# Top-p attention on one core: feature sums on another engine, the odd tile's work rearranged, diffusion a tile further ahead

## The chip, the core and the metric

The kernel runs on one core of one Trainium2 chip, in a single launch. The metric is the device time of a run in microseconds (us). A core has engines that each run their own queue of instructions: TensorE (matmul; PE, with its weight loads as PEld), VectorE (DVE), ScalarE (ACT), GpSimd (POOL) and SyncE (SP, which here only issues transfers). They wait for each other through semaphores.

## The reference, cut to what matters

`x` has 3327 nodes of 256 features, `adj` is a 3327 x 3327 matrix, everything in float32. Four layers run one after the other, each as `x = layernorm(x + layer(x, adj))`: a GraphSAGE layer, a GCN with a Mamba block behind it, a GAT, and the layer that the change touches:

```python
def top_p_attention(X):                    # A: 3327 x 3327
    q, k = X @ W1.T @ W2.T, X @ W3.T       # 64 columns each
    probs = softmax(q @ k.T)
    # per row: sort, keep the largest until their sum reaches 0.9
    A = probs * keep
    return A / max(A.sum(-1), 1e-12)

R = adj + eye(N); R = R / R.sum(-1)
Z, Xf, Xa = 0, X, X
for n in range(2):
    A = top_p_attention(Xa)
    Xf = R @ Xf                            # "diffusion"
    Xa = A @ Xa                            # "values"
    Z = Z + Xf @ U1[n].T + Xa @ U2[n].T
out = layernorm(X + Z)
```

The two rounds of this loop are called the first and the second attention here.

## The kernel before, in words

**Tiles.** The nodes are padded to 3328 and cut into `nt` = 26 row tiles of 128; two neighbouring tiles make one of `nh` = 13 pairs. A row tile of attention needs a row `e` of 3328 logits for each of its 128 nodes, in one SBUF buffer (`e`, four of them).

**One row tile of the first attention** goes through these steps. `scores` (line 1141) yields four chunks of 832 logits: two matmuls into the PSUM tile `sc`, of which there is one buffer, then a copy to `e` on ScalarE (line 1160; line 1163 where the last chunk is uneven). GpSimd sets the padded last column (line 1146). `search_short` (line 1387) finds the row's threshold on VectorE: 26 MAX8 over 128 columns each, given out in five steps (four steps of 5, one of 6), then six rounds of MAX8 and MATCH_REPLACE over the 208 candidates; in the first round it also issues the exponential of the whole row on ScalarE (line 1404). Then come `crossing`, which sums the sorted candidates to find the threshold `v`, and two passes over half of `e` each, which zero what lies under `v`. Every `yield` is one step, and `look()` takes one step of the search at the head of `queue`; a look where the queue is empty does nothing.

**Pairs and products.** Diffusion and values of a pair of tiles multiply a 256-row block matrix with the features by a scheme with seven 128-wide products in place of eight (`products`, line 1165), which needs sums of blocks on both sides. `blocks` (line 1191) makes the four sums of the feature blocks once, in `t1` to `t4` (in the buffer `G`, which is not in use yet), with four VectorE operations of 128 x 1664. The sums on the other side are made per pair: `diffused_pair` (line 1224) loads parts of the adjacency (`at`, two groups of 128 columns of each half to a part, and sums stored in `mixed` by an earlier layer) and adds the rest (`cb`) on VectorE; it yields once after its first part and once after each of its 13 groups of products. `assembled` (line 1176) puts the seven results together (`c`, eight VectorE operations), and `with_own` adds the own part, which `own_part` put in `F` on GpSimd (line 1203). `attended_pair` (line 1252) does the same for the values: `turn` transposes four 128 x 128 blocks of `e` on TensorE into the PSUM tile `tp` (two buffers) and ScalarE copies it to `wt` (line 1263); `mix` makes four sums of it in `sw` with three VectorE operations; then come seven matmuls. It begins with three turns and two mixes before its first yield; after that each of 13 steps issues the turn three ahead, one mix and one step's products. In the traces the three turns at its start are read from the matmuls `tp<-ident,e`.

`first` (line 1550) closes a row tile: the value sums are scaled, transposed to `xt` (VectorE copy), multiplied with U1 and U2, and stored (`s`, `Y`, `G` and the keys of the second attention).

**What sets the order.** In the first attention `fixed` is true: the wrapper `Fixed` (lines 882 to 893, where most matmuls and VectorE operations are recorded under line 891) keeps TensorE and VectorE in the order in which the program issues their instructions. So the order is written out by hand in a loop over pairs, and one engine's instruction that waits holds everything behind it on that engine. ScalarE, GpSimd and SyncE are ordered by the framework's scheduler, except for single instructions that are pinned.

Each turn of the loop (lines 1726 to 1745) has four parts. (1) The *even stage*, 7 steps: at each step one step of the next pair's diffusion (`spread`), at every second step one chunk of logits of tile 2i+2, looks as `counts` says; step 0 ends the previous pair (`end_pair`), step 5 empties the search queue and starts the values of pair i (`attend_to`, with the three turns). (2) Seven steps of values, with one look in five of them. (3) The *odd stage*, 6 steps of diffusion, with logits of tile 2i+3 at every second step, the second tile's `first`, and looks of 2, 1, 2, 1, 2, 1; the search of tile 2i+2 is emptied at its end and that of tile 2i+3 appended. (4) Six steps of values; the diffusion's assembly comes after the first, and the looks are in the last four.

```python
stage(spread, 7, logits(2 * i + 2), ends, counts,
      {0: lambda: end_pair(i - 1) if i else None, 5: lambda: attend_to(i)})
counts = [1, 2, 2, 2, 2, 0, 0]
```

Ahead of the loop an opening does the diffusion of tile 1 alone with plain products (`diffused_first`), between the logits of tiles 0 and 1, with the first search beside it. `blocks` comes ahead of all this.

**The second attention** (lines 1778 to 1839) goes tile by tile: in iteration `i` (from -2) tile `i+2` gets its logits, tiles `i` and `i+1` are searched (`search_long`, mostly on ScalarE and GpSimd), tile `i-1` has its values, and one tile's diffusion (`diffused`, line 1302: loads of `at`, 26 matmuls, one VectorE operation into `xf`) is spread through the iteration. Here the scheduler orders VectorE and TensorE too, except for what is pinned. `DL` is 1, and `more = range(len(xfs), min(nt, i + DL + 1))` gives iteration `i` the diffusion of tile `i+1`, from i = -1 to 24. Four buffers `xf` hold the results.

## Time and profile before

| | |
|---|---|
| three runs | 3424.53, 3426.78 (median), 3435.73 us |
| the profiled execution, its own time | 3433.03 us |
| its span, first to last instruction | 3431.1 us |
| mean granted TensorE clock | 0.964 |
| PE busy | 3140.4 us, 92% |
| PEld busy | 2565.8 us, 75% |
| DVE busy | 2686.5 us, 78% |
| ACT busy | 1735.4 us, 51% |
| POOL busy | 1127.6 us, 33% |
| first attention, about 1690 to 2568 us of the span | PE 840.35 of 878 us |
| second attention, about 2568 to 3431 us | PE 805.10 of 863 us |

How to read the profile. It shows one profiled execution, and its times start at the first instruction. An engine is busy while it runs an instruction; what an idle engine waited for is inferred from the semaphore that came last. In a line of a timeline the columns are the start, the duration, the engine, the source line, the operation, output <- inputs, the shape, how often it was repeated, and in square brackets the idle time ahead of it with its releaser. A table of windows has, for each stretch, its length and then every engine's busy time with its number of instructions. "PE tp L891 <- DVE e L891" in a list of waits reads: TensorE, about to write `tp`, waited for VectorE's last work on `e`; then come the total, the number of waits and the longest.

### The profile page before, as it was taken

The numbers are of one execution on the slowest core, as the hardware profiler recorded it, in microseconds if no ns is written. First come the engines' busy times: TensorE is split into PE (matmuls) and PEld (weight loads), VectorE is DVE, ScalarE is ACT, GpSimd is POOL, SyncE is SP. The second block draws the span as 40 slices with busy tenths as digits, with TensorE's granted clock in tenths as the row PEclk, the third lists the DMA queues.
The fourth block names the chain that finished last, engine by engine and source line by source line (L and its number), as shares of the span: only waits on it lengthen the run. The fifth ranks groups of instructions, "written<-read, shape, count | busy, mean of one in ns | idle before, by whom it ended". The sixth has DMA issues, their size and how long they took to land. (4 is left out here: it accounts for less than half of the span.)

```text
span 3431.1 us, 50276 instructions
## 1 busy us (share of the span) xinstructions
PE 3140.4 (92%) x18301; PEld 2565.8 (75%) x18301; DVE 2686.5 (78%) x5895; ACT 1735.4 (51%) x2764; POOL 1127.6 (33%) x1332
## 2 busy tenths in 40 slices
PE   8999888898988776999989999999998999999996
PEld 5999657676675554888778888888885677777775
DVE  4655368999999997877578778778755898988886
ACT  1000456767767675111133333333337788888883
POOL 0000245666665654111400000000003566656563
PEclk9999999999999988999999999999998999999998
DMA  6775334334343322444322232232213122222220
GB/s 200 251 253 188 105 101 125 110 108 116 102 115 89 69 57 81 150 137 151 115 76 87 65 88 79 69 89 80 71 50 102 52 68 68 64 66 65 72 64 16
DMA packets 206264, 344.31 MB, mean 100 GB/s; under 512 B 22223, under 2 KB 129167, under 8 KB 205871
## 3 DMA queue, kind: packets, MB, share of 16 engines
q1 hardware_dynamic: 205998, 340.92, 33.2%
q8 instruction: 148, 2.42, 0.3%
q14 instruction: 118, 0.96, 0.1%
HBM read 304.65 MB, written 36.21 MB: 99 GB/s over the span
## 5 line engine op out<-in xcount | busy, mean ns | idle before, releaser
L330 POOL TENSOR_TENSOR h<-du,row 128x2048 f32<-128x2048 f32 (+1 forms) x110 | 465.5, 4232 | 344.9 <-DVE hc L330 248.6
L330 DVE TENSOR_TENSOR_SCAN h<-dA,carry,h 128x512 f32<-128x512 f32 (+1 forms) x384 | 449.0, 1220 | 18.2 <-ACT dA L337 18.1
L337 ACT ACTIVATE dA<-t,A_log 128x512 f32<-128x512 f32 (+1 forms) x448 | 292.5, 658 | 147.1 <-DVE h L330 145.5
L1296 PE MATMUL acc<-F,at 128*128 128x256 f32 x1352 | 354.3, 388 | 1.8 <-DMA at<-in_adjT 1.8
L1341 PE MATMUL acc<-G,wt 128*128 128x256 f32 x1352 | 336.6, 392 | 9.7 <-ACT wt L1139 9.3
L1341 PEld LDWEIGHTS acc<-G,wt 128*128 128x128 f32 x1352 | 250.1, 193 | 72.4 <-ACT wt L1139 42.2
L1079 PE MATMUL acc<-F,at 128*128 128x257 f32 x1352 | 303.4, 381 | 0.7 <-ACT r L1023 0.7
L389 PE MATMUL cb<-F,at 128*128 128x256 f32 x1196 | 295.5, 395 | 8.0 <-ACT hn L409 3.4
L1296 PEld LDWEIGHTS acc<-F,at 128*128 128x128 f32 x1352 | 239.3, 191 | 74.9 <-issue 46.6
L1146 POOL MEMSET e<- 128x1 f32 x52 | 4.9, 99 | 838.5 <-PE tp L891 769.5
L1079 PEld LDWEIGHTS acc<-F,at 128*128 128x128 f32 x1352 | 253.3, 190 | 36.2 <-issue 1.0
L680 PE MATMUL y<-ident,hc 128*128 128x128 f32 x1664 | 236.4, 296 | 46.2 <-DVE hc L330 46.1
L680 PEld LDWEIGHTS y<-ident,hc 128*128 128x128 f32 x1664 | 210.4, 154 | 87.4 <-DVE hc L330 62.6
L389 PEld LDWEIGHTS cb<-F,at 128*128 128x128 f32 x1196 | 229.8, 198 | 58.3 <-issue 19.4
L330 DVE TENSOR_TENSOR hc<-h,row 128x2048 f32<-128x2048 f32 (+2 forms) x114 | 243.2, 2135 | 11.3 <-PE y L680 4.3
L891 PE MATMUL acc<-X,at 128*128 128x128 f32 (+1 forms) x988 | 173.7, 287 | 6.0 <-issue 6.0
L1263 ACT COPY wt<-tp 128x512 f32<-128x512 f32 x156 | 90.8, 589 | 166.6 <-PE tp L891 153.2
L138 PE MATMUL acc<-t,cb 128*128 128x128 f32 (+1 forms) x1014 | 168.4, 275 | 0.0
L891 PEld LDWEIGHTS acc<-X,at 128*128 128x128 f32 x988 | 142.2, 193 | 29.9 <-issue 26.1
L891 PE MATMUL acc<-G,sw 128*128 128x128 f32 x936 | 155.5, 275 | 0.0
L891 DVE MAX8 cand<-e 128x8 f32<-128x128 f32 x676 | 139.8, 277 | 5.0 <-ACT e L1160 3.2
L1160 ACT COPY e<-sc 128x832 f32<-128x832 f32 x78 | 65.9, 845 | 149.2 <-PE sc L891 149.1
(414 smaller groups left out, 7263.0 us busy)
## 6 DMA issues: line engine op xcount, KB each, us to landing
at<-in_adjT SPq DMA_DIRECT2D x54, 832.0 KB, 4.5
at<-in_adjT SPq DMA_DIRECT2D x130, 320.0 KB, 3.0
row<-bc SPq DMA_DIRECT2D x80, 512.0 KB, 5.1
at<-in_adjT SPq DMA_DIRECT2D x52, 640.0 KB, 5.5
at<-in_adjT SPq DMA_DIRECT2D x52, 576.0 KB, 4.1
at<-in_adjT SPq DMA_DIRECT2D x72, 256.0 KB, 3.1
at<-mixed SPq DMA_DIRECT2D x72, 256.0 KB, 3.6
mixed<-cb SPq DMA_DIRECT2D x26, 640.0 KB, 4.2
```

The source lines that it names most:

```text
L138: mm = nc.tensor.matmul(acc, w[:, j, :], x, start=(y == 0 and k % 3 == 0 and k < 6), stop=(y == nh - 1 and k in (2, 6)))
L330: return lambda *x, **k: tc.keep_in_program_order(op(*x, **k))
L337: decays.append(op(*x, **k))
L389: ten.matmul(acc, at[:, j % JC, :], X0[:, j, :], start=(j == 0), stop=(j == nt - 1))
L680: x = ten.matmul(y[:, g * P:(g + 1) * P], h[:, g, i * P:(i + 1) * P], ident, is_transpose=True, start=(first and g == 0), stop=(last and g ...
L891: return lambda *x, **k: tc.keep_in_program_order(op(*x, **k))
L1079: nc.tensor.matmul(acc, at[:, j, :], F[:, j0 + j, :], start=(j0 + j == 0), stop=(j0 + j == nt - 1))
L1146: nc.gpsimd.memset(e[:, n:], NEG)
L1160: copy(halves[:, :, c0:c0 + ws[0]], pl[:, :, :ws[0]])
L1263: nc.scalar.copy(wts[-1], pt)
L1296: nc.tensor.matmul(acc, at[:, j, :], rhs[:, j0 + j, :], start=(j0 + j == 0), stop=(j0 + j == nt - 1))
L1341: tensor.matmul(acc, wt[:, j, :], rhs[:, j0 + j, :], start=(j0 + j == 0), stop=(j0 + j == nt - 1))
```

## The change

Five edits.

1. `blocks` issues its four subtractions on GpSimd.
2. `attended_pair` yields after its first turn, after its second turn and first mix, and after its third turn and second mix, in place of once after all of them. A new `go_on` takes the next of these steps.
3. `stage` counts the keys of `then` from its end and takes a new argument `every` (2 unless given) for the logits. Even stage: the values start at its sixth step, `go_on` comes in its seventh step and once more behind it (after the remaining logits and ends); its looks become 2, 2, 2, 1, 0, 0, 0. Odd stage: one chunk of logits at every step (four chunks in steps 0 to 3, each `scores` yield being a chunk), the search of tile 2i+3 is appended at step 4 and the looks are 2, 2, 2, 2, 3, 3, with no `finish` behind it. The last values of the pair have a look in steps 2 and 5 only.
4. In the opening two chunks of tile 0's logits are issued ahead of the first diffusion's first step, and `blocks` is called behind tile 0's logits.
5. In the second attention iteration `i` diffuses tile `i+2`, from i = -2 to 23, one tile to an iteration; `xf` has five buffers.

```diff
         def blocks(x, t):
...
-            vector.tensor_sub(t1, b12, b11)
-            vector.tensor_sub(t2, b22, t1)
-            vector.tensor_sub(t3, b22, b12)
-            vector.tensor_sub(t4, t2, b21)
+            for y, c, d in ((t1, b12, b11), (t2, b22, t1), (t3, b22, b12), (t4, t2, b21)):
+                nc.gpsimd.tensor_tensor(y, c, d, op=ALU.subtract)
...
         def attended_pair(quads, psum, es, b):
...
-            for j in range(3):
-                turn(j)
-            for j in range(2):
-                mix()
+            turn(0)
+            yield None
+            turn(1)
+            mix()
+            yield None
+            turn(2)
+            mix()
             yield None
...
         def diffused(work, atp, psum, p, it, out, each=J3):
...
-            d = work.tile([P, D], F32, name="xf", bufs=DL + 3)
+            d = work.tile([P, D], F32, name="xf", bufs=DL + 4)
...
-                b = blocks(X, [flat[:, k * nh * HD:(k + 1) * nh * HD].rearrange("p (t d) -> p t d", t=nh) for k in range(4)])
...
-                def stage(spread, steps, groups, ends, counts, then):
+                def stage(spread, steps, groups, ends, counts, then, every=2):
                     for k in range(steps):
                         next(spread, None)
-                        then.get(k, int)()
-                        if k % 2 == 0:
+                        then.get(k - steps, int)()
+                        if k % every == 0:
                             next(groups, None)
...
+                def go_on():
+                    next(turned[0])
...
                 groups = logits(0)
                 x = diffused_first(quads, psum, 1, xfs)
+                next(groups)
+                next(groups)
                 for _ in groups:
                     next(x)
+                b = blocks(X, [flat[:, k * nh * HD:(k + 1) * nh * HD].rearrange("p (t d) -> p t d", t=nh) for k in range(4)])
...
                 for i in range(nh - 1):
-                    stage(spread, 7, logits(2 * i + 2), ends, counts,
-                          {0: lambda: end_pair(i - 1) if i else None, 5: lambda: attend_to(i)})
-                    counts = [1, 2, 2, 2, 2, 0, 0]
+                    stage(spread, len(counts), logits(2 * i + 2), ends, counts,
+                          {-7: lambda: end_pair(i - 1) if i else None, -2: lambda: attend_to(i), -1: go_on})
+                    go_on()
+                    counts = [2, 2, 2, 1, 0, 0, 0]
                     queue.append(searches[2 * i + 2])
...
-                    stage(spread, 6, logits(2 * i + 3), todo[1], [2, 1, 2, 1, 2, 1], {})
-                    finish()
-                    queue.append(searches[2 * i + 3])
+                    stage(spread, 6, logits(2 * i + 3), todo[1], [2, 2, 2, 2, 3, 3],
+                          {-2: lambda: queue.append(searches[2 * i + 3])}, 1)
...
-                        looks(k > 1)
+                        looks(k in (2, 5))
...
-                    more = range(len(xfs), min(nt, i + DL + 1))
+                    more = range(len(xfs), min(nt, i + DL + 2, len(xfs) + 1))
```

## The prediction, made before the changed kernel had run

> **What bounds the kernel now.** I read the page first (busy shares), then the engines' busy time by stage, then TensorE's own waits, then the timeline of one pair of tiles on TensorE, VectorE and ScalarE. The change touches two stages: the first attention (about 1690 to 2568 us of the span) and the second (2568 to 3431).

> By stage, the columns are the window, its length, then busy time and instruction count of PE, PEld, DVE, ACT and POOL, the granted clock and the DMA:

> ```profile
> 1948.82:2014.12 65.30, 64.00 (x496) 56.96 (x496) 52.19 (x177) 24.17 (x39) 0.20 (x2) 1.00 0.27 79
> 2014.12:2471.26 457.14, 448.04 (x3472) 398.72 (x3472) 365.10 (x1233) 169.99 (x273) 1.38 (x14) 1.00 0.27 79
> ```

> The first attention repeats every 65.30 us, one pair of tiles (457.14 is seven of them), and TensorE works 64.00 us of that. So at most 1.30 us a pair can be won in the steady part. TensorE's waits say where it is (total, times, longest):

> ```profile
> PE tp L891 <- DVE e L891: 21.9, 13, 8.9
> PE sc L891 <- ACT e L1160: 3.1, 2, 2.2
> PE tp L891 <- ACT wt L1263: 2.6, 11, 0.2
> ```

> ```profile
> 2012.57 0.49 PE L891 MATMUL tp<-ident,e 128*128 128x128 f32 x3
> 2014.12 0.76 PE L891 MATMUL tp<-ident,e 128*128 128x128 f32 x5 [1.06 <-DVE e L891]
> 2015.13 0.66 PE L891 MATMUL tp<-ident,e 128*128 128x128 f32 x4 [0.24 <-ACT wt L1263]
> ```

> The three turns of a pair stand in a row; the fourth transpose needs the odd tile's search, which ends 1.06 us late, and the third turn waits 0.24 us for a PSUM buffer. Eleven pairs do this; the first waits 8.86 and 1.33 us. VectorE is 80% busy (52.19 of 65.30), so its order matters. This is the odd stage on VectorE:

> ```profile
> 1974.40 0.69 DVE L891 COPY xt<-tp 128x512 f32<-128x512 f32 x1 [3.76 <-PE tp L891]
> ...
> 1978.55 0.43 DVE L891 TENSOR_TENSOR s<-tp,X 128x256 f32<-128x256 f32 x1 [1.49 <-PE tp L891]
> ...
> 1984.44 0.42 DVE L891 TENSOR_TENSOR sw<-wt 128x256 f32<-128x256 f32 x1
> 1984.90 0.62 DVE L891 TENSOR_TENSOR sw<-sw,wt 128x128 f32<-128x128 f32 x2
> ...
> 1988.56 0.42 DVE L891 TENSOR_TENSOR sw<-wt 128x256 f32<-128x256 f32 x1
> ...
> 1993.09 2.99 DVE L891 MAX8 cand<-e 128x8 f32<-128x128 f32 x15
> ```

> It stands still before `xt` and `s`, waiting for TensorE, then runs without a break into the sums `sw` (mix 9 at 1984.44, mix 10 at 1988.56) that TensorE's products 9 and 10 use. On ScalarE an exponential sits ahead of a copy of logits:

> ```profile
> 1968.14 3.07 ACT L1404 ACTIVATE e<-e,neg 128x3328 f32<-128x3328 f32 x1 [1.95 <-DVE neg L891]
> 1971.21 0.83 ACT L1160 COPY e<-sc 128x832 f32<-128x832 f32 x1
> ```

> [...] while VectorE waits 3.76 us for `xt`, nothing behind it runs. [...] here the 8.86 us wait is followed by half clock, the 1.06 us ones are not. [...] a GpSimd sum of 256 columns (L1588) took 4.09 us beside a VectorE pass over e, against 0.72 us at its shortest. [...] the 2048-column rows of L330 took 4.23 on average.

> **Part by part, in the first attention.**

> Sums of blocks on GpSimd. Four operations of 1664 columns leave VectorE (2.07, 1.98, 1.88 and 2.08 us: 8.0 us, 1702.4 to 1710.4). [...] GpSimd is free of the layer before at 1692.4, earlier than VectorE, and the first product that reads them starts at 1732; the own parts that fill GpSimd now (23 in 26.5 us) would still end by 1733. VectorE gains almost nothing at once: after the sums it waits 0.79 us more for a transfer before `cb` at 1711.16, which stays ahead of the search. [...] if the memset of e's last column, now at 1718.8, slipped to 1733, the first search would slip with it. I take zero, with +4 us as the bad end.

> Opening order. With two groups of logits ahead of the diffusion's first transfer, tile 0's logits end some 5.5 us sooner (before, the last copy ended at 1719.2). But VectorE then meets `F` behind TensorE's last diffusion product (1728.95, gap 5.79), in both orders. By then the new order has five rounds of the search done instead of one, so four rounds of 0.85 us come off what is behind, plus the rest of the shift: 4 to 7 us sooner at the first turn. I take -5.

> Turns spread out. One turn, then a product, turn, logits, turn: the 0.24 us goes, and twelve transposes find their copies. That is -0.24 x 11.

> Search of the odd tile earlier. Its looks move from values' steps (four to two) and from the even stage (9 before the turn to 7), so 2.9 us of VectorE work (six MAX8 of 0.195 us, two rounds of 0.85) leaves the stretch before the turn, against a lateness of 1.06 us. The wait goes: -1.06 x 11. Together with the turns -14.3 us.

> What it costs. Four groups of logits now follow each other at every step of the odd stage. The second (TensorE ready at 1969.48 + 1.65 = 1971.13) needs the one PSUM buffer of logits, whose copy stands behind the 3.07 us exponential and ends at 1972.04: a wait of 0.95 us a pair, where now there is none. If ScalarE were ordered copy first, the exponential would hold the next copy for about 0.6, so 0.6 to 1.0.

> The larger one: steps 4 and 5 of the odd stage hold all 26 MAX8 of the odd tile's search (26 x 0.195 = 5.1 us), in VectorE's queue *ahead of mix 9*. Count from TensorE's start of the product at 1978.35. Now VectorE finishes mix 9 at +7.15 (1985.5), and TensorE needs it at +11.0 (product 9, 1989.37) plus 0.45. Afterwards VectorE does 5.1 more and 0.4 less (one MAX8 of a round moves ahead of `s`): +11.85. TensorE comes earlier, because two groups of logits of 0.98 moved ahead: product 9 starts at +9.05, and its fourth operand, the last sum of the mix, is due at +9.7. Wait 2.1 us. Then VectorE has the eight operations of `c` and the two of `F` (1985.43 to 1988.64, 3.2 us) before mix 10 (1.05): +16.0. TensorE, released at +11.85, is through with product 9 at +12.75 and needs mix 10 at +13.2. Wait 2.75 us. Mix 11 and 12 then come in time. The idle time before `xt` and `s` doesn't absorb the MAX8, since they stand behind both. Sum 0.95 + 2.1 + 2.75 = 5.8 us a pair in eleven pairs; in the first pair no `xt` or `s` stops VectorE, and the same count leaves 1.3.

> First attention: 11 x 5.8 + 1.3 - 14.3 - 5 = +46. If those waits are a third shorter (TensorE slower on the way, VectorE a little faster than I add up) it is +25. Two waits near 2.5 us within 6.5 may also cost half-clock stretches of 3.4 us, each worth 1.7: 0 to +15; I take none.

> **The second attention.**

> ```profile
> 2568.80:2639.20 70.40, 54.40 (x208) 35.09 (x208) 27.66 (x80) 51.07 (x42) 27.54 (x60) 0.84 0.41 128
> 3342.60:3373.30 30.70, 25.51 (x127) 20.73 (x126) 26.31 (x78) 21.05 (x20) 13.56 (x32) 0.96 0.13 39
> ```

> One tile of diffusion (52 halves of 0.22, 11.5 us) moves from the iteration at 3342 to the opening at 2568. At the end VectorE is busy 26.31 of 30.70 us, so taking 11.5 us from TensorE wins only about 3: what is late next is the search of the last tiles. The opening has 16 us of idle TensorE, so the tile fits, but TensorE and ScalarE run in order there: the first transfer is issued at 2571.7 and takes 3 to 5 us, so logits behind its products come up to 7 us later, and the first searches with them. A cost of 0 to 10; I take 6. Net +3. One more `xf` buffer costs no time. SyncE's queue issues the same loads, one iteration earlier.

> **Sum.** The profiled execution took 3433.0 us (span 3431.1 and 1.9 around it). 46 + 3 = +49 gives 3482; the median of the runs, 6.2 lower, gives **3476**.

> **Rivals.** (a) VectorE keeps up, because the 13 us it has free in each pair take the MAX8 in: the waits at products 9 and 10 stay away, the logits' wait too. For it: 80% busy; against it: the free time lies ahead of `xt` and `s`. Then -14.3 - 5 + 3 = -16: about 3411. It decides once VectorE enters the odd values less than 4 us behind TensorE. (b) A part: only product 9 or the logits wait, about 1.3 us a pair, which cancels the turn's gain: 3420 to 3437. (c) The sums on GpSimd come late and hold TensorE's first products and the search: up to +10 on top of the main case. (d) The second attention's opening loses nothing and its end wins 3: main case at 3467.

> **How the numbers follow.** Main case (with c and d inside it) 0.74, own range 3447 to 3500: low end +25 first attention with -3 in the second, high end with half-clock stretches. Rival a 0.17, b 0.09. The range 3418 to 3500 leaves out most of (a) and the main case's tail. About 0.3% (10 us) can be told from no change: faster 0.17, same 0.08, slower 0.75.

> **What would show it.** Right: a pair lasts 69 to 70 us instead of 65.30; the wait for e before the turn is gone; new waits of TensorE for `sw` of some 2 and 2.7 us in each odd stage's values, and of `sc` on ScalarE's copy near 0.95. Wrong: a period at 64.0, or VectorE's MAX8 of the odd tile lying in the gap ahead of `xt`. The opening is right if the first turn comes about 5 us sooner; the second attention if its first turn comes 6 us later after 2568 and its last iterations 3 us shorter.

## The result: slower by more than forecast

The changed kernel takes **3512.56 us** (median of four runs, 3511.76 to 3516.53), the kernel before 3427.79 us in the same comparison: a ratio of 1.0246, 95% interval 1.0227 to 1.0265. Forecast were 3476 us and a range of 3418 to 3500; the sign was right, the time lies above the range. The profiled span grew from 3431.1 to 3510.6 us.

First TensorE's waits in the first attention of the changed kernel (the total in us, times, longest):

```profile
PE acc L891 <- DVE sw L891: 39.9, 43, 1.9
PE sc L891 <- ACT e L1160: 27.4, 15, 14.4
PE acc L891 <- DVE cb L891: 5.2, 1, 5.2
PE tp L891 <- DVE e L891: 4.9, 2, 3.4
```

The wait for `e` ahead of the turn is gone from every pair (two are left, in the opening), and a wait for the sums `sw` has come in its place, as forecast. But a single wait for logits of 14.4 us is new as well; nothing of that kind was in the forecast's sum. This is TensorE and VectorE in one odd stage and the values behind it:

```profile
2065.26 0.97 PE L891 MATMUL sc<-kT,q 64*128 64x416 f32 x4 [0.78 <-ACT e L1160]
...
2079.93 5.12 DVE L891 MAX8 cand<-e 128x8 f32<-128x128 f32 x26
2084.97 0.41 DVE L891 TENSOR_TENSOR sw<-wt 128x256 f32<-128x256 f32 x1
...
2085.43 0.49 PE L891 MATMUL acc<-G,sw 128*128 128x128 f32 x2 [1.39 <-DVE sw L891]
...
2089.55 0.49 PE L891 MATMUL acc<-G,sw 128*128 128x128 f32 x2 [1.86 <-DVE sw L891]
```

The 26 MAX8 of the odd tile's search stand directly ahead of the sums `sw` that TensorE waits for. Now three pairs by stretch, from one odd tile's `xt` to the next:

```profile
1929.67:2000.37 70.70, 66.35 (x498) 58.90 (x498) 52.33 (x176) 24.34 (x40) 0.20 (x2) 0.98 0.25 72
2000.37:2069.50 69.13, 64.78 (x499) 57.33 (x498) 52.23 (x176) 24.41 (x40) 0.20 (x2) 1.00 0.26 74
2069.50:2138.58 69.08, 64.72 (x498) 57.27 (x498) 52.23 (x176) 24.36 (x40) 0.20 (x2) 1.00 0.26 74
```

A pair takes 69.1 us where the granted clock (third number from the end) stays at 1.00, and 70.7 to 71.0 where it drops to half for 3.41 or 6.83 us (half clock, below); it was 65.3. VectorE's busy time is the same as before (52.2 us), only its order is new.

Cut at four marks that both traces have, the added time lies here:

| stretch | before | after | added | forecast |
|---|---|---|---|---|
| first logits to the `xt` in the odd stage of the loop's second turn (opening, first pair) | 143.3 | 160.0 | **+16.6** | -5 |
| from there ten pairs, to the `xt` in the odd stage of the last turn | 653.1 | 701.5 | +48.4 | 10 x 4.5 = +45 |
| from there to the second attention's first logits | 71.9 | 75.4 | +3.5 | +5.8 |
| second attention's first logits to the first product of its values | 72.2 | 85.3 | **+13.1** | +6 |
| from there to the end | 790.1 | 789.7 | -0.5 | -3 |

With the first logits 1.7 us earlier in the new trace (a difference of the layers ahead, which the change doesn't touch) that is the 79.4 us of the span. The pairs came as forecast; the two openings did not.

**The opening of the first attention.** In the kernel before, GpSimd set the column in time, and TensorE's longest wait for the copy of logits was 2.17 us:

```profile
1718.81 0.18 POOL L1146 MEMSET e<- 128x1 f32 x4
1718.82 3.39 DVE L891 MAX8 cand<-e 128x8 f32<-128x128 f32 x17 [1.79 <-ACT e L1163]
1726.88 0.97 PE L891 MATMUL sc<-kT,q 64*128 64x416 f32 x4 [2.17 <-ACT e L1160]
```

GpSimd, VectorE, ScalarE and TensorE of the changed kernel, in this order:

```profile
1715.45 3.71 POOL L1196 TENSOR_TENSOR G<-X,G 128x1664 f32<-128x1664 f32 x1
1719.10 3.70 POOL L1196 TENSOR_TENSOR G<-X 128x1664 f32<-128x1664 f32 x1
1722.74 3.70 POOL L1196 TENSOR_TENSOR G<-G,X 128x1664 f32<-128x1664 f32 x1
1726.36 0.20 POOL L1146 MEMSET e<- 128x1 f32 x4
```

```profile
1726.52 0.30 DVE L891 MAX8 cand<-e 128x8 f32<-128x128 f32 x1 [12.16 <-POOL e L1146]
```

```profile
1727.53 3.07 ACT L1405 ACTIVATE e<-e,neg 128x3328 f32<-128x3328 f32 x1 [16.00 <-POOL F L1201]
1730.60 0.83 ACT L1160 COPY e<-sc 128x832 f32<-128x832 f32 x1
```

```profile
1715.05 1.99 PE L891 MATMUL acc<-X,at 128*128 128x256 f32 x8
1731.48 1.76 PE L891 MATMUL sc<-kT,q 64*128 64x416 f32 x4 [14.44 <-ACT e L1160]
```

It is a queue four engines long. A memset (0.20 us for four of them) stands behind three sums of 3.70 us in GpSimd's queue; the first sum stands ahead of the own parts, at 1691.1. The last of 26 MAX8 reads the column that it sets and waits 12.16 us for it. The exponential needs that MAX8 (it starts 0.12 us after `neg`, which the MAX8 leads to; GpSimd's next own part, which the profile names, merely ended later than `neg`), and the copy of the next tile's logits stands behind the exponential on ScalarE. TensorE needs the one PSUM buffer that this copy frees, and it runs in program order, so the diffusion's products behind the logits stand still too.

**The opening of the second attention**, on TensorE:

```profile
2635.58 0.97 PE L1154 MATMUL sc<-kT,q 64*128 64x416 f32 x4 [1.93 <-ACT q L907]
2645.68 2.90 PE L1297 MATMUL acc<-F,at 128*128 128x256 f32 x6 [9.13 <-DMA at<-in_adjT]
2648.51 1.76 PE L1154 MATMUL sc<-kT,q 64*128 64x416 f32 x4
```

After one chunk of tile 0's logits the first diffusion's products are next in TensorE's order; their load is issued at 2638.53, and they start at 2645.68. Tile 0's other chunks wait behind them: the second starts 12.9 us after the first, where it was 2.7 us before. In the kernel before, the diffusion came after tile 0's logits, and the load landed beside those:

```profile
2571.43 1.76 PE L1154 MATMUL sc<-kT,q 64*128 64x416 f32 x4 [0.99 <-ACT e L1139]
...
2581.31 5.14 PE L1296 MATMUL acc<-F,at 128*128 128x256 f32 x12
```

### The profile page after: what moved, and what is told of

Read it like the earlier page. It is cut to its first block, busy times and chain, and to the rows that moved or that the text cites. A ratio compares the mean times of both kernels' runs of the same rounds, so it can differ in the third digit from the quotient of the medians.

```text
span 3510.6 us, 50279 instructions
## 1 busy us (share of the span) xinstructions
PE 3163.3 (90%) x18301; PEld 2583.3 (74%) x18301; DVE 2678.9 (76%) x5891; ACT 1738.0 (50%) x2764; POOL 1136.5 (32%) x1336
## 5 line engine op out<-in xcount | busy, mean ns | idle before, releaser
L330 POOL TENSOR_TENSOR h<-du,row 128x2048 f32<-128x2048 f32 (+1 forms) x110 | 465.8, 4235 | 344.6 <-DVE hc L330 248.5
L330 DVE TENSOR_TENSOR_SCAN h<-dA,carry,h 128x512 f32<-128x512 f32 (+1 forms) x384 | 448.9, 1220 | 18.3 <-ACT dA L337 18.1
L1297 PE MATMUL acc<-F,at 128*128 128x256 f32 x1352 | 353.5, 388 | 11.2 <-DMA at<-in_adjT 11.1
L1342 PE MATMUL acc<-G,wt 128*128 128x256 f32 x1352 | 336.7, 392 | 13.2 <-ACT wt L1139 12.9
L330 DVE TENSOR_TENSOR hc<-h,row 128x2048 f32<-128x2048 f32 (+2 forms) x114 | 243.0, 2133 | 11.3 <-PE y L680 4.3
L891 PE MATMUL acc<-G,sw 128*128 128x128 f32 x936 | 163.1, 284 | 36.6 <-DVE sw L891 36.6
L891 PE MATMUL acc<-X,at 128*128 128x128 f32 (+1 forms) x988 | 176.6, 291 | 0.0
L891 PEld LDWEIGHTS acc<-X,at 128*128 128x128 f32 x988 | 143.9, 195 | 32.3 <-issue 27.5
L891 PEld LDWEIGHTS acc<-G,sw 128*128 128x128 f32 x936 | 134.9, 199 | 41.3 <-DVE sw L891 41.3
L891 DVE MAX8 cand<-e 128x8 f32<-128x128 f32 x676 | 137.7, 276 | 12.3 <-POOL e L1146 12.2
```

Of the source, the lines that this page charges most:

```text
L330: return lambda *x, **k: tc.keep_in_program_order(op(*x, **k))
L891: return lambda *x, **k: tc.keep_in_program_order(op(*x, **k))
L1297: nc.tensor.matmul(acc, at[:, j, :], rhs[:, j0 + j, :], start=(j0 + j == 0), stop=(j0 + j == nt - 1))
L1342: tensor.matmul(acc, wt[:, j, :], rhs[:, j0 + j, :], start=(j0 + j == 0), stop=(j0 + j == nt - 1))
```

## The experiments

Ratios are to the kernel before, run in the same comparison (its medians there were 3430.35 to 3431.86 us).

**E1 to E4 start from the changed kernel.** E1 puts the memset ahead of the sums; on TensorE, VectorE and ScalarE every instruction keeps its place in the order. (All four sums then stand behind the own parts, the first one too.)

```diff
-                nc.gpsimd.memset(e[:, n:], NEG)
+                first_memset.append(nc.gpsimd.memset(e[:, n:], NEG))
...
-                b = blocks(X, [...])
+                with tc.issue_after(first_memset[0].ins): b = blocks(X, [...])
```

> The changed kernel, with the memset of e's last column put ahead of the four sums in GpSimd's queue; nothing else moves. In the changed kernel the last MAX8 of the first search waited 12.17 us for that memset (1726.5 us) and the exponential behind it held the copy of logits, so TensorE waited 14.4 us. Theory (the queue behind the sums is what made the opening slow): that wait is gone, the opening is 11 to 15 us shorter, about 3499. Rival (the opening is slow because VectorE and TensorE meet later anyway, at the assembled diffusion or at cb): under 4 us come back, 3509 to 3513.

Measured: 3498.27 us, ratio 1.0192 (1.0175 to 1.0209). The four sums still end at 1725.4. GpSimd in this kernel:

```profile
1710.55 0.10 POOL L1146 MEMSET e<- 128x1 f32 x1
1710.61 7.39 POOL L1196 TENSOR_TENSOR G<-X 128x1664 f32<-128x1664 f32 x2
1717.95 3.70 POOL L1196 TENSOR_TENSOR G<-X,G 128x1664 f32<-128x1664 f32 x1
```

The wait of 14.4 us is down to 2.7 and the first row of the table is 148.4 us in place of 160.0: 11.5 us were the memset's place in the queue. That is the theory. (The medians differ by 14.3 us; in the traces the rest is 1.9 us in the ten pairs, where five half-clock stretches are left of six, and 1.2 us in the layers ahead.) It leaves 5.1 us above the kernel before, where the forecast had a gain; the section on the prediction comes back to it.

**E2** undoes the second attention's edit alone.

```diff
-                    more = range(len(xfs), min(nt, i + DL + 2, len(xfs) + 1))
+                    more = range(len(xfs), min(nt, i + DL + 1))
```

> The changed kernel with the second attention as it was (diffusion one tile ahead, four xf buffers). Theory from the traces: the opening of the second attention lost 13.1 us and its end won 0.4, so about 12.7 us come back: 3500. Prediction's count: opening 6, end 3, so 3 us come back: 3510.

Measured: 3501.18 us, ratio 1.0198 (1.0181 to 1.0215). The second attention's opening is back at 70.5 us. The theory's 12.7 us fit, the forecast's 3 do not.

**E3** moves the MAX8 of the odd tile's search out of the odd stage.

```diff
-                    stage(spread, 6, logits(2 * i + 3), todo[1], [2, 2, 2, 2, 3, 3],
+                    stage(spread, 6, logits(2 * i + 3), todo[1], [2, 2, 2, 2, 0, 0],
...
-                        looks(k in (2, 5))
+                        looks((0, 1, 1, 2, 2, 2)[k])
```

> The changed kernel with the six looks of the odd stage's last two steps (26 MAX8 and one round) moved into the values' steps behind it; the number of looks ahead of the turn stays. Theory (these MAX8 stand ahead of mix 9 and 10): TensorE's waits for sw, 3.6 us a pair with 1 us of refill, and the half-clock stretches behind them go; 4.5 to 5.5 us a pair in 11 pairs, 3452 to 3465. Rival (VectorE has too much to do wherever the MAX8 stand): the waits move to later sums or to the turn, under 20 us come back, over 3492.

Measured: 3498.30 us, ratio 1.0200 (1.0183 to 1.0217). The theory's number was wrong, and the rival's (over 3492) came in. The waits for `sw` and the half-clock stretches in the ten pairs are gone and that for `sc` stays, but TensorE stands still three times at the start of the next even stage:

```profile
2088.95 0.49 PE L891 MATMUL acc<-G,cb 128*128 128x128 f32 x2 [0.93 <-DVE cb L891]
...
2092.59 0.44 PE L891 MATMUL tp<-ident,c 128*128 128x128 f32 x2 [0.99 <-ACT c L1554]
...
2095.93 2.43 PE L891 MATMUL tp<-U,xt 128*128 128x256 f32 x10 [1.33 <-DVE lim L891]
```

The first waits for the next diffusion's sum `cb`, the second for the scaled values `c` (ScalarE's, behind VectorE's assembly), the third are the products that read `xt`. A pair takes 68.5 us. So here eight looks close together make VectorE late for what comes next; the odd stage's last steps were not the only bad place for them.

**E4** keeps all looks and takes one chunk of logits from behind the exponential (`stage` takes a list of steps as `every`).

```diff
-                          {-2: lambda: queue.append(searches[2 * i + 3])}, 1)
+                          {-2: lambda: queue.append(searches[2 * i + 3])}, (0, 2, 3, 4))
```

> The changed kernel with the odd stage's four chunks of logits at steps 0, 2, 3, 4 in place of 0, 1, 2, 3, so that the second does not stand behind the exponential. Theory (the waits add): 0.78 us a pair and its refill go, 11 x 0.85 = 9 us, 3503. Rival (VectorE sets the end of the odd stage): the wait for sw grows by what the wait for sc loses, no change, 3512.

Measured: 3488.76 us, ratio 1.0168 (1.0151 to 1.0185): more than either expected. A pair without half clock takes 67.2 us, 1.9 less. TensorE in one pair:

```profile
2074.46 0.49 PE L891 MATMUL acc<-G,sw 128*128 128x128 f32 x2 [0.30 <-DVE sw L891]
2075.12 0.49 PE L891 MATMUL acc<-X,sw 128*128 128x128 f32 x2 [0.17 <-DVE sw L891]
...
2078.58 0.69 PE L891 MATMUL acc<-G,sw 128*128 128x128 f32 x2 [1.86 <-DVE sw L891]
```

The wait for `sc` (0.78) is gone, and the first wait for `sw` fell from 1.39 to 0.30, because a chunk of logits (0.97 us of TensorE) now stands behind `s`: VectorE's mix 9 starts 15.46 us after `xt` in both kernels, and TensorE is ready for it 1.1 us later than it was. The second stays at 1.86: released by mix 9, TensorE meets VectorE's eight operations of `c` and two of `F` ahead of mix 10.

**E5 to E7 start from the kernel before**, with small parts of the change. E5 has the spread turns alone (edit 2, with `go_on` in the even stage's last step and behind it).

> The kernel before with the second edit alone: the values' three first turns spread over three steps, everything else as before. Theory: what stands ahead of TensorE's fourth transpose on VectorE stays, so the wait for e (1.06 us a pair) stays and only the wait for wt (0.24 us, with refill up to 0.6) goes: 3 to 7 us faster, a pair 64.7 to 65.1 us. Rival (spreading makes VectorE's first two mixes late for the first products): a new wait for sw at each pair's start, no gain or slower.

Measured: 3428.61 us, ratio 0.9989 (0.9979 to 0.9998); a pair takes 64.85 us in place of 65.30. The wait for `wt` is gone, that for `e` is nearly the same (1.05). Eleven pairs make 5 us of it, as expected; the interval of the times holds 1 to 7.

**E6** gives the values one more look: `looks(k > 0)` for `looks(k > 1)`.

> The kernel before with one more look of the odd tile's search in the values behind the odd stage (five in place of four); so 1.2 us of MAX8 leaves the stretch ahead of the turn. Theory (a small shift fits where the whole of 26 MAX8 does not): the 1.06 us wait for e goes, nothing else waits: 10 to 12 us faster. Rival (VectorE is late at c and F there too): the wait moves to the diffusion's cb or the scaled values c, within 4 us of no change.

Measured: 3425.78 us, ratio 0.9986 (0.9979 to 0.9993); a pair takes 64.90 us. The wait for `e` fell from 1.06 to 0.48, not to nothing. VectorE stands waiting for TensorE ahead of the even tile's `s` (1.8 us before, 1.3 now), so only the work between `s` and the end of `e` counts, and that fell by 0.56 us, from 6.82 to 6.26. That is 0.4 us a pair, 4 to 5 us in all, half of what was expected.

**E7** has both.

> The kernel before with both: the three turns spread and one more look in the values. Theory: both small waits of the turn go, a pair takes 64.0 to 64.2 us, 12 to 15 us faster than before. Rival: as for the single edits, no gain.

Measured: 3421.86 us, ratio 0.9973 (0.9960 to 0.9986); a pair takes 64.44 us. TensorE's waits in the pairs are one line:

```profile
PE tp L891 <- DVE e L891: 4.9, 10, 0.5
```

Both parts add, to less than was expected (12 to 15 us), since the wait for `e` is halved and not gone. The turn's gain can be had, then, without the rest of the change.

**E8**, from the changed kernel, lets the second attention's iteration -2 diffuse nothing and iteration -1 two tiles.

```diff
-                    more = range(len(xfs), min(nt, i + DL + 2, len(xfs) + 1))
+                    more = range(len(xfs), min(nt, i + DL + 2) if i > -2 else 0)
```

> The changed kernel, with no diffusion in the second attention's iteration -2 and two tiles of it in iteration -1; still one tile further ahead from there on. Theory (what the opening lost is the wait of TensorE, in order, for the first load of the adjacency, with tile 0's logits queued behind it): the loss goes but for what the second tile displaces, 0 to 4 us; 8 to 13 us faster than the changed kernel, 3500 to 3505. Rival (the extra 11.5 us of products are themselves on the path): no faster than the changed kernel, 3510 to 3515.

Measured: 3499.16 us, ratio 1.0200 (1.0174 to 1.0226). The opening takes 71.5 us in place of 85.3, and the wait for the load is 0.7 us in place of 9.1. Up to its end it holds 186 of the diffusion's products, where the changed kernel has 208 and the kernel before 156. The whole second attention, with all products in it, takes 858 us in E8's trace (its fastest execution) against 875 in the changed kernel. So 30 products more than before cost nothing in the opening; where TensorE met their load was the cost.

**E9**, from the kernel before: the sums on GpSimd alone (edit 1), called where they were.

> The kernel before with the first edit alone: the four sums of feature blocks on GpSimd, called where they were. Theory (on GpSimd the sums stand ahead of the memset of e's last column): the first search waits for the memset until about 1727 us of the span, where it had it at 1718.8, so the exponential and the logits behind it come 5 to 8 us later, 4 to 9 us slower than before. The prediction's count: 0. Rival (taking 8 us from VectorE ahead of the first search pays): 2 to 5 us faster.

Measured: 3439.36 us, ratio 1.0023 (1.0014 to 1.0031). GpSimd:

```profile
1716.88 3.72 POOL L1196 TENSOR_TENSOR G<-X,G 128x1664 f32<-128x1664 f32 x1
1720.56 3.70 POOL L1196 TENSOR_TENSOR G<-X 128x1664 f32<-128x1664 f32 x1
1724.21 3.69 POOL L1196 TENSOR_TENSOR G<-G,X 128x1664 f32<-128x1664 f32 x1
1727.84 0.19 POOL L1146 MEMSET e<- 128x1 f32 x4
```

The same order on GpSimd, so edit 1 by itself does it (TensorE waits 8.8 us for the copy of logits); the table's first row is 151.3 us against 143.3, and the pairs are unchanged at 65.30.

**E10**, from the kernel before: the odd stage's edit alone (logits at every step, the search appended at step 4, the changed kernel's looks in all four parts).

> The kernel before with the odd stage's edit alone: logits at every step, the search appended at step 4, looks 2, 2, 2, 2, 3, 3 there, two in the values and 2, 2, 2, 1 in the even stage; sums, turns, opening and second attention as before. Theory (this edit alone makes the pair longer): waits for sc near 0.8 and for sw near 3.6 us, the wait for e gone, so a pair takes 69 to 70 us without half-clock stretches and the time is 43 to 60 us above before. Rival (the cost needs the spread turns, which put mixes later): a pair under 67 us.

Measured: 3497.92 us, ratio 1.0191 (1.0173 to 1.0209), 66 us more than before, where 43 to 60 were expected without half clock. The waits are those of the changed kernel (0.78 for `sc`, 1.39 and 1.86 for `sw`). A pair takes 69.6 us without half clock, but seven of ten have it and take some 71.2, which makes 11 to 12 of the 66 us.

**E11 and E12** look for the best version. E11 is E7 with the second attention of E8; E12 has a look in each of the six values' steps besides (`looks(1)`).

> The kernel before with the three turns spread, five looks of the odd tile's search in the values (in place of four), and the second attention's diffusion a tile further ahead with two tiles in iteration -1. Theory: 8.7 us from the first two as measured, and the 3 us that the second attention's later part was shorter in the run with two tiles at -1: 10 to 13 us faster than before. Rival (the 3 us are noise of one profile, or the opening takes them): 7 to 9 us faster.

> The same with a look in every one of the six values' steps, so that the first round of the search and its exponential lie there too. Theory (the wait of 0.48 us for e that five looks leave goes as well): 4 to 6 us faster than with five looks. Rival (as with the MAX8 all in the values, VectorE is late at the next diffusion's cb and at the scaled values c): no faster than with five looks, or slower.

Measured: E11 3419.29 us, ratio 0.9963 (0.9950 to 0.9975), the lowest time here and 0.25 to 0.5% faster than before; its interval overlaps that of E7, so the second attention's part in it is not shown by the times. In its trace the second attention from the first values on is 3.3 us shorter than before, won with the first three tiles (84.5 us against 92.9) and partly given back later; but E12 has the same second attention, and its trace has 790.6 us there against 790.1 before. E12: 3431.92 us, ratio 0.9998 (0.9989 to 1.0008). The wait for `e` is gone, and two others came in its place in each pair:

```profile
PE tp L891 <- DVE xt L891: 3.9, 10, 0.4
PE sc L891 <- ACT e L1160: 3.4, 10, 0.3
```

The third row of the table is also 5.6 us longer (78.1 against 72.5). There the exponential has moved ahead of a copy to `wt` that TensorE needs, at the start of the last pair's values:

```profile
2509.92 3.07 ACT L1407 ACTIVATE e<-e,neg 128x3328 f32<-128x3328 f32 x1 [7.15 <-DVE neg L891]
2512.99 0.56 ACT L1332 COPY wt<-tp 128x512 f32<-128x512 f32 x1
2513.61 2.93 PE L891 MATMUL acc<-X,wt 128*128 128x256 f32 x6 [4.39 <-ACT wt L1332]
```

In E11 that wait is 0.28 us and the exponential comes 3.2 us after the products' start.

## Why the prediction was wrong

**The pair: mechanism right, the sum right in part by luck.** Forecast were +5.8 of waits and -1.3 of the turn, 4.5 us a pair. The trace has a wait for `sc` of 0.78 (forecast 0.95), at mix 9 1.39 + 0.17 (2.1) and at mix 10 1.86 + 0.16 (2.75), 4.4 us in all. The turn's 1.3 us are gone as forecast, and TensorE's busy time is 0.7 us longer (64.7 against 64.0; two products on `sw` behind a wait are recorded with 0.49 us, without one with 0.39, which some of the expectations call refill): a pair at full clock is 3.8 us longer. "Two waits near 2.5 us within 6.5 may also cost half-clock stretches ... I take none" was the wrong choice. The trace of the kernel before has a stretch of that length too (clock 0.50 from 2698.61 to 2702.03, in the second attention); that waits of 2.5 us would bring them no trace showed yet. In the changed kernel half clock came six times in ten pairs, for 3.41 or 6.83 us, and cost 1.6 or 1.9 us each time, 10.5 us, which made up for the smaller waits; that +48.4 lies so near +45 is luck. E10 shows that the odd stage's edit alone does all this, E7 that the spread turns and one earlier look are worth 0.86 us a pair by themselves, of the 1.3 forecast. Rival (a), VectorE keeps up, did not come in: the waits for `sw` are in every pair, and E3 moved these MAX8 to one other place and found VectorE late there too.

**"Sums of blocks on GpSimd ... I take zero, with +4 us as the bad end"** is the step that failed most. The text even named the case, "if the memset of e's last column, now at 1718.8, slipped to 1733, the first search would slip with it", and then put nothing for it into the sum: not the wait of VectorE (12.16 us), nor the exponential, copy and TensorE behind it. The 4 us of the bad end come with no working. It asked whether the own parts "would still end by 1733", its author's estimate; what matters is who stands behind the sums, not when they end. The price of a sum was not what failed: L330's 2048-column operations took 4.53 us on average (80 of them; the forecast's 4.23 is the mean with 30 of 1536 columns), 1664/2048 of that is 3.68 us, and 3.70 were measured. E1 puts 11.5 us on the memset's place, E9 finds 8 with edit 1 alone. Rival (c) came nearest, with up to 10 us on top of the main case: the search was held, at 11.5 us. TensorE's first products, which it named too, did not wait for the sums; what held TensorE was the copy of logits.

**"Opening order ... I take -5"** failed too, by some 6 us. With the memset out of the way (E1) the fourth transpose of the first turn is released 55.9 us after the first logits, against 55.0 before: nothing won. Five rounds of the search were indeed done ahead of `F`, and the turn's wait (8.89 us in the trace; the forecast has 8.86) fell to 3.7. But the chunks issued one behind the other wait for each other's copies (2.35 and 0.94 us), and VectorE then takes 20 MAX8 of tile 1 ahead of a `cb`, which TensorE awaits for 5.05 us:

```profile
1737.20 3.96 DVE L891 MAX8 cand<-e 128x8 f32<-128x128 f32 x20
1741.08 0.67 DVE L891 TENSOR_TENSOR cb<-at 128x512 f32<-128x512 f32 x1
```

These two lines are E1's VectorE. The forecast took rounds off "what is behind" and didn't ask what VectorE would be late for next. No run has the opening's edit alone, so this account is read from E1's trace. The other 4.2 us of E1's 5.1 come after that transpose. They are mostly the odd stage's edit in the first pair: E10, with the old opening, has 3.7 there. The forecast had 1.3 of waits against 1.3 of the turn.

**"A cost of 0 to 10; I take 6"** for the second attention's opening: measured 13.1. The first load was given 3 to 5 us (in the kernel before, 320 KB loads of `at` took 3.0 us in the median of 95 from 2700 to 3300 us, and 5.5 in the median of eight from 2570 to 2600); it landed 6.9 us after its issue (7.4 in the kernel before, 7.1 in E8), the first product started 7.1 us after it (2638.53 to 2645.68), and TensorE, with one chunk done, had nothing else in its order for 9.13 us. E8 loses the wait. **"wins only about 3"** at the end: 0.5 measured from the first values on. Between traces of the same second attention this stretch varies by more: the seven with the old one have 790.1 to 793.8 us, the changed kernel, E1, E3 and E4 789.4 to 789.7. So some 2 us may have been won, but not at the end: the last three tiles take 73.5 us, against 72.0 before and 72.0 to 74.7 in the other six. The 11.5 us taken out of TensorE's work come back as waiting there. TensorE's waits in the last 110 us, of the kernel before and then of the changed one:

```profile
PE tp L1327 <- DVE e L1540: 4.7, 1, 4.7
PE acc L1341 <- ACT wt L1139: 3.8, 3, 3.1
PE tp L1327 <- DVE e L1534: 2.6, 1, 2.6
```

```profile
PE acc L1342 <- ACT wt L1139: 9.4, 4, 5.1
PE tp L1328 <- DVE e L1541: 7.6, 1, 7.6
PE tp L1328 <- DVE e L1535: 5.6, 1, 5.6
```

11.1 us before, 22.6 after: the difference is the tile that was moved away. Two of the three kinds of wait are for `e`, the search's product; the forecast had said that the search comes next, yet it kept 3 us.

In sum, the first row of the table is 21.6 us off: 11.5 the memset, some 6 the opening's order, some 4 the first pair. With the second attention's 9.6 that is the miss of 30 us between +49 and the +79.4 of the span; what the other rows are off nearly cancels. One sum on the side is wrong too: without the opening's 6 us the main case is 3470 us, where rival (d) has 3467.

## What to carry to other kernels

Work that moves to a lightly used engine goes into a queue. List the small operations that will stand behind it, and follow each through every engine that waits for it before calling the move free. On an engine that runs in program order, a rearrangement is worth what the tightest next operand leaves: one look earlier won time (E6: a pair of 64.90 us for 65.30), six moved together lost more than they freed in both places where they were tried (69.1 us, and 68.5 in E3). Work moved from ahead of a wait for the other engine may win nothing: in E6 only what lay behind VectorE's last such wait counted (0.56 us of work gone there, 0.58 off TensorE's wait). And where the first products of a stage need a load, put work that is ready ahead of them in the order (the wait for the load was 9.1 us in the changed kernel, 0.7 in E8).

## What the runs showed of the hardware

```profile
1874.64 0.49 PE L891 MATMUL acc<-G,sw 128*128 128x128 f32 x2 [1.38 <-DVE sw L891]
1875.29 0.49 PE L891 MATMUL acc<-X,sw 128*128 128x128 f32 x2 [0.16 <-DVE sw L891]
```

```profile
1949.73 0.49 PE L891 MATMUL acc<-G,sw 128*128 128x128 f32 x2 [1.86 <-DVE sw L891]
1950.38 0.49 PE L891 MATMUL acc<-X,sw 128*128 128x128 f32 x2 [0.17 <-DVE sw L891]
```

The pairs cut into stretches of 3.4133 us at these multiples, and TensorE's idle time counted from the matmul records: the six stretches at full clock just ahead of half clock held 1.55 or 1.66 us of it, in pieces, and no other stretch at full clock held more than 1.54. No general limit is read from that: in the second attention of the same trace a stretch with 1.87 us (2709.40 to 2712.82) was not followed by half clock. In the kernel before, the wait of 8.89 us (1744.80 to 1753.69) goes with a clock of 0.50 from 1749.71 to 1759.95, and the waits of 1.06 us, one in each pair, with 1.00 throughout (1840 to 2490).

The count also goes with only some pairs being hit. A pair of 69.1 us is no multiple of 3.4133, so the waits lie otherwise on these stretches in each pair: in the hit pairs one holds 1.55 or 1.66 us of idle time, while in the two pairs from 2000.37 to 2138.58 the waits are divided, and the fullest hold 1.48 and 1.53. That this decides is the author's reading; no run isolates it.

Moving the sums also sped GpSimd up. In the kernel before, its own parts took up to 3.82 us each while VectorE's four sums ran (1702.4 to 1710.4), and 0.92 us in the median of all:

```profile
1692.38 26.49 POOL L1203 TENSOR_SCALAR F<-X,rdeg 128x256 f32<-128x256 f32 x23
```

In the changed kernel the same 23 take 20.8 us, none over 0.95. That is why E9's memset comes some 10 us later, counted from the first logits, and not by the full 14.8 us of the four sums.
